# Moving one of the five DMA issues per step pair from GpSimd to SyncE in the second attention of a hybrid block

## The chip, the cores and the metric

One core of a Trainium2 chip runs the whole kernel in one launch. The metric is device time in microseconds (us). A measurement of the kernel is the median of several runs; a profiled execution is one further run, whose trace gives the durations used below.

## The reference, cut to what matters

The input x has 4 batches of 1024 rows of 256 numbers, all in f32. Four layers are added to it in turn, each applied to a layer norm of x: an attention (a), a feed-forward net, a second attention (b) and the same feed-forward net again. "Layer 3" is the second attention.

```
x = x + attn_a(layernorm(x)); x = x + ffn(layernorm(x))
x = x + attn_b(layernorm(x)); x = x + ffn(layernorm(x))

# attn_b(x): 16 heads of 64
h = layernorm(x) * ln_scale + ln_bias
q = (h @ w_down_q.T) @ w_up_q.T ; k, v = from (h @ w_down_kv.T)
q, k = rope(q), rope(k)
out = softmax(q @ k.T / 8) @ v
return out @ w_out.T + x
```

## The kernel before, in words

**Tiling.** An attention is walked in 256 steps: 4 batches, 8 pairs of heads in each, 8 tiles of 128 queries in each pair of heads. A step computes the scores of 128 queries against 1024 keys for two heads, in one PSUM tile `sc` for each head. Two steps, 2h and 2h+1, make a step pair h, and there are 128 step pairs. A period below is the time of one step pair.

**What a step does.** `scores` (L238, TensorE) fills the two `sc` tiles. `exponentials` takes the row maximum (L249, VectorE) and the exponential with its sum (L251, ScalarE) into `p`; `invert` (L259 VectorE, L260 ScalarE) adds the inverse sums to it. `turn` (L271, VectorE) transposes `p` into `T`, but only within blocks of 32x32. To complete the transpose, 16 squares of `T` (a square is 32 partitions x 1088 f32, 136 KB, for a whole step pair) must move to another group of 32 partitions, in a tile `pT`. `send` (L289 to L295) does this with one DMA per square. `weigh` (L304, TensorE) multiplies `pT` with the values, `take` (L314 ScalarE, L316 GpSimd) copies the sums out of PSUM and scales them by the inverse sums, `project` (L167 TensorE, L326 ScalarE, L328 GpSimd) multiplies with the output weights and adds the result to x.

**Squares in layer 3.** `attention` is called with kept=1 there, so the square (0, 0), which stays in its partitions, is copied by ScalarE (`keep`, L287), and 15 squares are left in the list `sent`. SyncE (SP) issues the first ten, GpSimd (POOL) the last five (POOL_DMA = 5). In layer 1, kept is 0 and there are 16: SP issues eleven and GpSimd five.

**Order of the work.** The kernel is scheduled by hand: each engine executes its instructions in the order in which the loop `steps_with` emits them. In a step s that is: `invert(s)`; `scores(s+1)`; if s is even, GpSimd's sends of step pair s/2-1, then `project` of step pair (s-6)/2; `exponentials(s+1, 0)`; if s is odd, `weigh` of step pair (s-5)/2; `exponentials(s+1, 1)`; if s is odd, `take`; `turn(s)`; if s is odd, SP's sends of step pair (s-1)/2. So SP's sends follow straight after the second transpose of a step pair, and GpSimd's come in the next step. `weigh` of a step pair comes four steps after the second transpose.

**Buffers.** `T` and `pT` have two buffers each. `turn(2h+4)`, the first transpose into the buffer of T of step pair h, can start only when all transfers of step pair h have landed. SP's first send of step pair h can start only when `take` of step pair h-2 has read pT (L316). The scores have three PSUM tiles.

**Other work on the two queues.** In layer 3, SP also issues the loads of the next pair of heads' weights: three of `wo` (L212, L214) and three of `w` (L636), once in four step pairs each. GpSimd also does, in nearly every step pair, one block of the rope: two DMAs that swap neighbouring partitions into a tile `turned` (L652), and a step later three elementwise operations (L657, L658, L659), the first of which overwrites what those DMAs read and so waits until they have landed. GpSimd's order in a period is therefore L316, two L652, five L295, L328, L657, L658, L659.

**Completion semaphores.** SP's DMAs take eight completion semaphores in turn, and GpSimd's another eight; an issue waits for the transfer that used its semaphore before.

Of the kernel before, what the change touches and what calls it, by code (L numbers as in the profile page):

```python
# [27 lines left out]
HB = 2  # L28
# [4 lines left out]
POOL_DMA = 5  # L33
# [6 lines left out]
def hybrid_block_kernel(  # L40
# [5 lines left out]
    nc = tc.nc  # L46
# [134 lines left out]
    def attention(prep_batch, prep_pair, wo, loader, lead, kept):  # L181
# [47 lines left out]
        def scores(s):  # L229
            g, qs = steps[s]  # L230
            qT, kT = tiles[g]["qT"], tiles[g]["kT"]
            for j in range(2):
                sc[s, j] = ps_sc.tile([P, S], F32, tag="sc", name="sc")
            for m in range(S // 512):
                for half in range(2):
                    for j in range(2):
                        rows = slice(j * DH, (j + 1) * DH)
                        nc.tensor.matmul(  # L238
                            sc[s, j][ts(half, DH), ts(m, 512)],
                            qT()[rows, ts(2 * qs + half, DH)], kT()[rows, ts(m, 512)],  # L240
                            start=True, stop=True,
                        )

        def exponentials(s, j):
            if j == 0:
                probs[s] = pp.tile([P, NK, NG, SQ], F32, tag="p", name="p")
                total[s] = small.tile([P, 2], F32, tag="total", name="total")
            nmax = small.tile([P, 1], F32, tag="nmax", name="nmax")
            nc.vector.tensor_reduce(nmax, sc[s, j], AX.X, ALU.max, negate=True)  # L249
            place = j ^ (s % HB)  # L250
            nc.scalar.activation(  # L251
                probs[s][:, :NK2, ts(j, 2), :],
                sc.pop((s, j)).rearrange("p (k c i) -> p k c i", c=2, i=SQ), AF.Exp,
                bias=nmax, accum_out=total[s][:, place : place + 1],
            )

        def invert(s):
            t = total.pop(s)
            nc.vector.reciprocal(t, t)  # L259
            nc.scalar.copy(  # L260
                probs[s][:, NK2].rearrange("p (j c) i -> p j (c i)", j=2),
                t.unsqueeze(2).to_broadcast([P, 2, DH]),
            )

        def turn(s):
            h, q = divmod(s, HB)
            if q == 0:
                T[h] = tp.tile([P, SENT], F32, tag="T", name="T").rearrange(
                    "p (c q k i) -> p c q k i", c=NG, q=HB, k=NK
                )  # L270
            nc.vector.transpose(  # L271
                T[h][:, :, q, :, :].rearrange("p c k i -> p k c i"), probs.pop(s)
            )
# [8 lines left out]

        sent = [ac for ac in squares if ac not in [(a, a) for a in range(kept)]]

        def keep(h):
            for a in range(kept):
                nc.scalar.copy(pT[h][ts(a, SQ), a], T[h][ts(a, SQ), a])  # L287

        def send(h, engine, which):  # L289
            if h not in pT:  # L290
                pT[h] = ptp.tile([P, SENT], F32, tag="pT", name="pT").rearrange(
                    "p (a q k i) -> p a q k i", a=NG, q=HB, k=NK
                )
            for a, c in which:
                engine.dma_start(pT[h][ts(c, SQ), a], T[h][ts(a, SQ), c])  # L295

        def weigh(h):

            v = tiles[HB * h // NT]["v"]()
            av[h] = [group(P) for q in range(HB)]  # L300
            for k in range(NK2):
                for q in range(HB):
                    for j in range(2):
                        nc.tensor.matmul(  # L304
                            av[h][q][ts(j ^ q, DH)], v[ts(j, DH), k, :],
                            pT[h][ts(j, DH), :, q, k, :],
                            start=(k == 0), stop=(k == NK2 - 1),
                        )

        def take(h):  # L310

            oT[h] = otp.tile([P, HB, P], F32, tag="oT", name="oT")
            for q, sums in enumerate(av.pop(h)):
                nc.scalar.copy(oT[h][:, q], sums)  # L314
            parts = oT[h].rearrange("p q (a i) -> p a q i", i=SQ)
            nc.gpsimd.tensor_mul(parts, parts, pT.pop(h)[:, :, :, NK2, :])  # L316

        def project(h):
            g, t0 = divmod(HB * h, NT)
            b, pr = pairs[g]  # L320
            po = group(HB, D)
            for t in range(HB):
                paired(po[:, t, :], [(oT[h][:, t], [wos[g][:, t]] * 2)])
            oT.pop(h)
            got = tmp.tile([P, HB, D], F32, tag="tmp", name="got")
            nc.scalar.copy(got, po)  # L326
            xd = xs[b][:, t0 : t0 + HB, :]
            nc.gpsimd.tensor_add(xd, xd, got)  # L328

        def steps_with(others):  # L330
            for k, f in others:
                pieces.setdefault(k, []).append(f)
            for s in range(-1, n + LAG + 1):
                h, part = divmod(s - LAG, HB)
                ahead = 0 <= s + 1 < n
                if 0 <= s < n:
                    invert(s)
                if ahead:
                    scores(s + 1)
                if part == 1 and 0 <= s // HB - 1 < n // HB:  # L340
                    send(s // HB - 1, nc.gpsimd, sent[len(sent) - POOL_DMA :])
                if part == 1 and 0 <= h < n // HB:
                    project(h)
                if ahead:
                    exponentials(s + 1, 0)
                for f in pieces.get(s - EARLY, ()):
                    f()
                if part == 0 and 0 <= h < n // HB:
                    weigh(h)
                if ahead:  # L350
                    exponentials(s + 1, 1)
                if part == 0 and 0 <= h < n // HB:
                    take(h)
                if 0 <= s < n:
                    turn(s)
                if part == 0 and 0 <= s // HB - 1 < n // HB:
                    keep(s // HB - 1)
                    T.pop(s // HB - 1)
                if part == 0 and 0 <= s < n:
                    send(s // HB, nc.sync, sent[: len(sent) - POOL_DMA])  # L360
                for f in pieces.get(s, ()):
                    f()

# [128 lines left out]
    def layer_a():  # L492
# [70 lines left out]
        later = [(4 + i, lambda i=i: rows.measure(2 + i // TQ, i % TQ)) for i in range(6 * TQ)]  # L563
        later += [(4 + 6 * TQ, lambda: rows.finish[2]())]
        first, steps = attention(batch_a, pair_a, wo_a, nc.gpsimd, lead=3, kept=0)
        loads, xn, pair = first[:2], first[2:14], first[14:]

# [16 lines left out]
    def layer_b(rows):  # L584
# [45 lines left out]
        def pair_b(b, pr):  # L630
# [47 lines left out]
            return {name: lambda name=name: made[name] for name in ("qT", "kT", "v")}, load, work  # L678

        return attention(batch_b, pair_b, wo_b, nc.sync, lead=5, kept=1)  # L680


# [73 lines left out]
```

## Time and profile before

| | us |
|---|---|
| median of 3 runs | 3288.75 (3285.65 to 3289.74) |
| profiled execution, its own time | 3283.29 |
| its span, first to last instruction | 3281.4 |
| granted TensorE clock, mean | 0.996 of full speed |

How the page is read: a group's busy time is the union of its instructions, "idle before" is the time in which the engine stood still just before them and what ended that; the chain is followed back from the last instruction to whatever released it. SP has no busy row, since all that it does is waiting and issuing; its rows carry the name SPq. The span has four parts: layer 1 from 0 to about 1480 us, a first feed-forward net to about 1680 us, layer 3 to about 3030 us, and the second feed-forward net to the end. The rows of the page on the transfers are these:

```
pT<-T SPq DMA_DIRECT2D x2688, 136.0 KB, 4.7
pT<-T POOLq DMA_DIRECT2D x1280, 136.0 KB, 4.7
turned<-kT POOLq DMA_DIRECT2D x128, 128.0 KB, 3.5
turned<-qT POOLq DMA_DIRECT2D x128, 128.0 KB, 3.3
```

The first is 128 x 11 of layer 1 and 128 x 10 of layer 3, and the last column is the median time from issue to landing in us.

### The profile page before, as it was taken

To read this page: it belongs to the slowest core of one execution; us is meant where nothing else is said; L and a number is where in the kernel's file an instruction comes from. 1 tells how busy PE (TensorE), PEld (TensorE's weight loads), DVE (VectorE), ACT (ScalarE), POOL (GpSimd) and SP (SyncE) were. 2 spreads that over 40 slices of the span, in tenths; PEclk is the share of its full clock that TensorE was granted. 3 is DMA by queue.
4 is the path that set the end of the run, shared out by engine and by line. 5 is a ranking of instruction groups with operands and counts; after the bars stand their busy time and mean duration, and the time that the engine had idled before them with its cause. 6 is when DMAs were issued, how large, how long until landed. Compare 5 with 4: busy or idle time off the path is not lost.

```text
span 3281.4 us, 126564 instructions
## 1 busy us (share of the span) xinstructions
PE 3201.6 (98%) x52736; PEld 2022.3 (62%) x52736; DVE 2531.3 (77%) x2386; ACT 2109.0 (64%) x4304; POOL 1958.4 (60%) x2738
## 2 busy tenths in 40 slices
PE   8999999999999999999999999999999999998999
PEld 4666666666666666666555556666656666665666
DVE  7988888888888888941049889998989999998100
ACT  5666666666666666642447777777778777777332
POOL 4544454545444445430159888998989999996110
PEclk9999999999999999999999999999999999999999
DMA  8888888888888888840029889998888899998100
GB/s 226 224 220 213 226 223 222 219 227 223 222 214 218 222 229 225 218 116 0 2 81 237 223 217 240 242 240 236 240 229 240 240 243 247 245 246 214 38 20 20
DMA packets 244697, 642.13 MB, mean 196 GB/s; under 512 B 74304, under 2 KB 102976, under 8 KB 244128
## 3 DMA queue, kind: packets, MB, share of 16 engines
q1 hardware_dynamic: 161104, 397.60, 47.6%
q0 software_dynamic: 83024, 236.44, 25.8%
q8 instruction: 419, 6.86, 0.9%
q14 instruction: 150, 1.23, 0.1%
HBM read 43.39 MB, written 4.19 MB: 15 GB/s over the span
## 4 chain that ended last, share of the span: by engine, by line
PE 78%; SPq 8%; DMA 5%; DVE 3%; ACT 3%; issue 3%; POOL 1%; DVEq 0%; POOLq 0%; ACTq 0%
PE sc L238 23%; PE mm L304 21%; PE mm L167 16%; SPq L295 7%; PE mm L421 7%; PE ph L410 7%; PE mm L176 5%; DMA pT<-T 4%; DVE T L271 1%; DVE nmax L249 1%; ACT p L251 1%; PE mm L153 1%; POOL oT L316 0%; ACT gT L414 0%; SPq L214 0%
## 5 line engine op out<-in xcount | busy, mean ns | idle before, releaser
L249 DVE TENSOR_REDUCE nmax<-sc 128x1 f32<-128x1024 f32 x1024 | 1204.5, 1218 | 226.7 <-PE sc L238 223.5
L251 ACT ACTIVATE p<-sc,nmax 128x1024 f32<-128x1024 f32 x1024 | 1145.3, 1119 | 324.0 <-DVE nmax L249 324.0
L271 DVE STREAM_TRANSPOSE T<-p 128x2176 f32<-128x2176 f32 x512 | 1247.1, 2436 | 41.0 <-DMA pT<-T 17.6
L238 PE MATMUL sc<-kT,qT 64*64 64x512 f32 x8192 | 1085.5, 599 | 16.0 <-ACT p L251 10.6
L304 PEld LDWEIGHTS mm<-pT,v 64*64 64x64 f32 x32768 | 950.3, 133 | 145.6 <-issue 103.4
L304 PE MATMUL mm<-pT,v 64*64 64x128 f32 x32768 | 984.5, 269 | 14.5 <-issue 13.5
L295 POOL DMA_DIRECT2D pT<-T x1280 | 629.6, 499 | 121.1 <-PE sc L238 56.2
L316 POOL TENSOR_TENSOR oT<-oT,pT 128x256 f32<-128x256 f32 x256 | 186.1, 727 | 718.7 <-ACT oT L314 636.3
L238 PEld LDWEIGHTS sc<-kT,qT 64*64 64x64 f32 x8192 | 333.1, 133 | 409.9 <-issue 277.1
L328 POOL TENSOR_TENSOR x<-x,got 128x512 f32<-128x512 f32 x256 | 330.9, 1293 | 27.8 <-ACT got L326 23.9
L326 ACT COPY got<-mm 128x512 f32<-128x512 f32 x256 | 150.0, 586 | 283.0 <-PE mm L167 282.9
L428 DVE TENSOR_TENSOR x<-x,mm 128x512 f32<-128x512 f32 x32 | 22.0, 687 | 367.2 <-PE mm L421 367.1
L167 PE MATMUL mm<-wo,oT 128*64 128x256 f32 x2048 | 278.4, 393 | 19.6 <-POOL oT L316 18.6
L167 PEld LDWEIGHTS mm<-wo,oT 128*64 128x64 f32 x2048 | 124.6, 136 | 266.4 <-POOL oT L316 217.4
L414 ACT ACTIVATE gT<-ph,b_sb 128x512 f32<-128x512 f32 x128 | 87.5, 686 | 301.9 <-PE ph L410 301.8
L260 ACT COPY p<-total 128x128 f32<-128x128 f32 x512 | 151.8, 296 | 195.4 <-DVE total L259 188.5
L167 PE MATMUL mm<-hT,w 128*64 128x512 f32 x1024 | 242.9, 596 | 1.0 <-ACT hT L156 1.0
L421 PE MATMUL mm<-w_sb,gT 128*128 128x256 f32 x1024 | 226.0, 381 | 6.6 <-ACT hT L156 6.6
L410 PE MATMUL ph<-hT,w_sb 128*128 128x512 f32 x512 | 230.2, 603 | 0.5 <-ACT hT L156 0.5
L421 PEld LDWEIGHTS mm<-w_sb,gT 128*128 128x128 f32 x1024 | 193.1, 190 | 39.4 <-ACT hT L156 9.4
L396 POOL TENSOR_TENSOR x<-x,b_sb 128x256 f32<-128x256 f32 x64 | 44.5, 728 | 275.6 <-ACT xn L147 275.6
L251 ACT ACTIVATION_READ_ACCUMULATOR p<-sc,nmax 128x1 f32 x1024 | 205.3, 200 | 0.0
(90 smaller groups left out, 2473.1 us busy)
## 6 DMA issues: line engine op xcount, KB each, us to landing
pT<-T SPq DMA_DIRECT2D x2688, 136.0 KB, 4.7
pT<-T POOLq DMA_DIRECT2D x1280, 136.0 KB, 4.7
turned<-kT POOLq DMA_DIRECT2D x128, 128.0 KB, 3.5
turned<-qT POOLq DMA_DIRECT2D x128, 128.0 KB, 3.3
w<-in_wqkv_a POOLq DMA_DIRECT2D x96, 128.0 KB, 6.1
wo<-in_wo_a POOLq DMA_DIRECT2D x32, 128.0 KB, 5.4
wo<-in_wo_a POOLq DMA_DIRECT2D x64, 64.0 KB, 5.5
wo<-in_wo_b SPq DMA_DIRECT2D x32, 128.0 KB, 3.6
```

The lines of the kernel that those rows point to most:

```text
L167: nc.tensor.matmul(out[ts(j, DH)], lhsT[:, ts(j, DH)], rhs[j], start=(first and i == 0), stop=(last and i == len(parts) - 1),)
L176: nc.tensor.matmul(out[ts(j, DH)], lhsT, rhs[:, ts(j, DH)], start=(i == 0), stop=(i == len(parts) - 1),)
L238: nc.tensor.matmul(sc[s, j][ts(half, DH), ts(m, 512)], qT()[rows, ts(2 * qs + half, DH)], kT()[rows, ts(m, 512)], start=True, stop=True,)
L249: nc.vector.tensor_reduce(nmax, sc[s, j], AX.X, ALU.max, negate=True)
L251: nc.scalar.activation(probs[s][:, :NK2, ts(j, 2), :], sc.pop((s, j)).rearrange("p (k c i) -> p k c i", c=2, i=SQ), AF.Exp, bias=nmax, acc ...
L271: nc.vector.transpose(T[h][:, :, q, :, :].rearrange("p c k i -> p k c i"), probs.pop(s))
L295: engine.dma_start(pT[h][ts(c, SQ), a], T[h][ts(a, SQ), c])
L304: nc.tensor.matmul(av[h][q][ts(j ^ q, DH)], v[ts(j, DH), k, :], pT[h][ts(j, DH), :, q, k, :], start=(k == 0), stop=(k == NK2 - 1),)
L316: nc.gpsimd.tensor_mul(parts, parts, pT.pop(h)[:, :, :, NK2, :])
L328: nc.gpsimd.tensor_add(xd, xd, got)
L410: nc.tensor.matmul(ph, w1_sb[:, c, ts(f, P)], hT[n][:, c, :], start=(c == 0), stop=(c == NC - 1),)
L421: nc.tensor.matmul(po[n][:, t % 2, :], gT[n][:, f, ts(t, P)], w2_sb[:, f, :], start=(f == 0), stop=(f == NF - 1),)
```

## The change

The number of squares that GpSimd sends is POOL_DMA less the number of squares that ScalarE keeps. In layer 1 this is still five. In layer 3 it is four, and SP sends eleven. The square that changes its queue is the eleventh of the list `sent`, from partitions 64 to 95 to partitions 32 to 63; SP issues it straight after its ten others, where GpSimd issued it first of its five in the next step. Nothing else moves on any engine; SP's first send of a step pair waits for four of GpSimd's completion semaphores in place of five.

```diff
         sent = [ac for ac in squares if ac not in [(a, a) for a in range(kept)]]
 
+        by_pool = POOL_DMA - kept
+
...
                 if part == 1 and 0 <= s // HB - 1 < n // HB:
-                    send(s // HB - 1, nc.gpsimd, sent[len(sent) - POOL_DMA :])
+                    send(s // HB - 1, nc.gpsimd, sent[len(sent) - by_pool :])
...
                 if part == 0 and 0 <= s < n:
-                    send(s // HB, nc.sync, sent[: len(sent) - POOL_DMA])
+                    send(s // HB, nc.sync, sent[: len(sent) - by_pool])
```

## The prediction

> **What bounds the kernel now.** The change touches layer 3 alone, so I read the page first for what TensorE does over the span, then the window of layer 3 by itself (1700 to 2980 us, 122 periods of 10.5 us), then the waits of that window engine by engine, and last the records of the two queues. The page and the window, whose columns are PE, PEld, DVE, ACT and POOL busy, then clock, DMA share and GB/s:
>
> ```profile
> PE 3201.6 (98%) x52736; PEld 2022.3 (62%) x52736; DVE 2531.3 (77%) x2386; ACT 2109.0 (64%) x4304; POOL 1958.4 (60%) x2738
> ...
> PE 78%; SPq 8%; DMA 5%; DVE 3%; ACT 3%; issue 3%; POOL 1%; DVEq 0%; POOLq 0%; ACTq 0%
> ```
>
> ```profile
> 1700.00:2980.00 1280.00, 1245.70 (x23037) 784.18 (x23035) 1167.95 (x1014) 979.32 (x1961) 1136.93 (x1476) 0.99 0.89 237
> ```
>
> TensorE is busy for 1245.7 of 1280 us here: 34.3 us are all that any relief of another engine could give in this window. GpSimd (89%), VectorE (91%) and the DMA engines (0.89) are close behind, so the stage is nearly balanced. SP has no busy figure; summed from its records in the window it is 1189 us: 979.9 for 1215 sends of squares (mean 0.806), 117 for weight loads, some 90 for the gaps of 0.045 between instructions and for passed waits. That is 9.75 us a period, 93%, and leaves 0.74 us idle. Its issues and GpSimd's, by duration (min/median/max, ns):
>
> ```profile
> L295 SPq DMA_DIRECT2D pT<-T x1215: 507/598/2159, 1700.0 to 2976.9; - x174
> ```
>
> ```profile
> L295 POOL DMA_DIRECT2D pT<-T x605: 489/492/522, 1710.2 to 2975.3; - x152
> ```
>
> SP's shortest issues are near 0.59, and the mean is higher because the third to sixth of each ten take 0.83 to 1.08: these fall in the time of GpSimd's five. GpSimd's never lengthen. Now who waits, first TensorE, then GpSimd, then SP, then VectorE:
>
> ```profile
> PE mm L167 <- POOL oT L316: 15.4, 23, 3.3
> ```
>
> ```profile
> POOL kT L657 <- DMA turned<-kT: 8.9, 13, 1.1
> POOL qT L657 <- DMA turned<-qT: 8.3, 10, 1.4
> ```
>
> ```profile
> SPq L295 <- DVE total L259: 60.7, 51, 3.3
> SPq L295 <- POOL oT L316: 14.5, 14, 3.5
> ```
>
> ```profile
> DVE nmax L249 <- PE sc L238: 61.5, 109, 2.7
> ...
> DVE T L271 <- DMA pT<-T: 8.5, 11, 2.0
> ```
>
> About half of TensorE's idle time is for L316, the scaling on GpSimd; SP mostly waits for the transpose (named "total", the last instruction of the same semaphore); VectorE waits little for landings. The chain puts SP and the landings at 28% of this window. I discount that: many of its hops go from a landing to L316, but L316 reads a pT that `weigh` has already read in whole, and GpSimd's records show it busy without a gap up to such an L316. These hops are the last use of a shared semaphore, not a wait.
>
> **What GpSimd gains.** One issue of 0.492 us less in each of 128 step pairs, 63 us off its queue. Most has no one waiting. In the window, 13 of TensorE's gaps before L167 come with an L316 that started over 0.15 us after ScalarE's copy was done, because GpSimd was still at work; they sum to 12.4 us. (The other ten or so, 0.3 us each, have GpSimd waiting, and gain nothing.) One issue less starts L316 up to 0.49 us earlier, unless L657 must wait for the swapped tile:
>
> ```profile
> 2077.95 1.14 POOL L652 DMA_DIRECT2D turned<-kT  x2
> 2079.08 2.43 POOL L295 DMA_DIRECT2D pT<-T  x5
> 2081.53 1.28 POOL L328 TENSOR_TENSOR x<-x,got 128x512 f32<-128x512 f32 x1
> 2083.94 1.27 POOL L657 TENSOR_TENSOR kT<-kT,cos_sb 128x512 f32<-128x512 f32 x1 [1.13 <-DMA turned<-kT]
> ```
>
> The five sends and L328 are what covers the flight of the two swaps, 3.3 to 3.5 us. Here the cover was 1.13 us too short, and a shorter send row only lengthens that wait. Over 121 rotations of layer 3, 26 wait so now, and with 0.49 us less cover 61 would: in half the periods part of the gain or all of it is lost. Taking for each of the 13 gaps the least of 0.49 us, the gap itself and the cover to spare leaves 4.3 us: seven gaps with the whole 0.49, two with 0.36 and 0.46, four with nothing. I take -3 us, since the freed time is partly limited by what is next late (SP, or the transpose); the ends are 0 and -7 (all 13 gaps and the one at 2982 us, 0.49 us each at most).
>
> **What SP pays.** One more issue at the tail of its row. The nearest row is its tenth in layer 3, mean 0.788 us, with 0.045 of gap 0.83; the eleventh of layer 1's rows is near it, 0.727. Against this GpSimd's burst is one shorter. The ten issues of a row take 8.10 us, 2.2 more than ten of 0.59; put down to GpSimd's five, that is 0.44 each, and by issues three to six alone (1.5 us over 0.59 in all) 0.30. So the row lengthens by 0.83 less 0.30 to 0.44, about +0.45 us. The bounds are +0.1 (the transfer engines, not the issue, pace the row, and the 15 transfers are the same) and +0.83 (nothing comes back).
>
> Two statements of the Trainium skill, page "DMA: Bandwidth & Descriptors", speak for making the move freely. "Issuing engine by pattern" calls the hardware queue of SP generally faster than GpSimd's; the row differs here, 0.806 us against 0.492 an issue. "Issuing engines are not separate DMA queues" says that all queues end on the same 16 engines, and that the issue time saved by spreading is usually small beside the transfer. The first half would make the landing of the last square unchanged: cost 0. The second half doesn't hold here: in the window the DMA engines move 237 GB/s, so 136 KB takes 0.59 us at that rate, no more than its issue on SP. By the page the sum is -3 us; by the rows SP's queue is itself a resource with 0.74 us left, and the price below is added. I follow the rows.
>
> **Where the longer row goes.** Two things are queued behind it on SP: the weight loads, needed long after, and the next row. A row starts late when SP is still at work: now in the median 0.65 us after the transpose, where 0.13 is the least, and 1.1 to 1.2 us in the periods after loads. With 0.45 us more of work the idle 0.74 shrinks to about 0.3, and such lateness grows by some 0.3. So the last landing of a step pair, now in the median 12.3 us after the transpose, moves by 0.75 to 0.8. Who needs it? `weigh` starts 3.0 us after it (5% of the pairs: 0.6), so it hardly notices. The first transpose into the same T buffer, L271, starts 1.0 us after it, in 5% of the pairs 0.1 to 0.2. Shifting each of 115 step pairs' landings by 0.8 us gives VectorE 21 us of new waits. VectorE has 112 us idle in the window, 61.5 of them waiting for scores, and 6 of the 21 disappear there. Of the 15 left, most are covered too, because the PSUM tile that VectorE and ScalarE then free is needed only after a `weigh` of 3.5 us: subtracting the margin between each exponential's end and the scores that reuse its tile leaves 4.9 us on TensorE. The same working gives 1 us at a shift of 0.4, 14 at 1.2 and 25 at 1.5: cheap at first, steep past one microsecond.
>
> **Sum.** -3 from GpSimd, +5 from SP: +2 us. Against the profiled execution, 3283.3 becomes 3285.3. That execution lies 5.5 us under the median of the three runs, so the forecast is 3288.75 + 2, about 3291.
>
> **The rivals.** A measurement of this kernel can tell about 0.2%, 6.6 us, from no change.
>
> *Absorbed both ways* (likeliest, 0.50): the sum above, from -4 (shift 0.3, the whole of GpSimd's gain) to +6. About 3291.
>
> *SP becomes the bound* (0.38): the row lengthens by the full 0.83 us, so that SP needs 9.75 + 0.83 = 10.6 us a period where the others need 10.5; the place is the first transpose of a step pair on VectorE, waiting for the eleventh square. The point from which it decides is a growth of 0.74 us a row, SP's idle time. It then costs 0.1 us in each of 128 periods, 13 us, and with the shift of 1.2 us (14 us) to 1.5 us (25 us) less GpSimd's 3, between 8 and 22: about 3302. For it speaks that SP's work is uneven (loads of 1.6 to 1.9 us in every second period), so that it runs out of slack there first; against it, that the burst which slows SP shrinks.
>
> *GpSimd's relief wins* (0.12): SP's row grows by only 0.1, the transposes wait for nothing new, and the lateness that GpSimd carries over from one period to the next shrinks by more than one issue each time, -7 to -10: about 3281. For it speaks the row "PE mm L167 <- POOL oT L316", the largest of TensorE's waits; against it, the lost cover of the swaps.
>
> That the change doesn't do what it says is excluded by the order of instructions: GpSimd loses 128 issues and SP gains 128.
>
> **How the numbers follow.** The forecast is 3291, of the absorbed case, whose own range is 3284 to 3296. The range that should hold 8 in 10 must reach into the SP case and need not hold the fast one: 3283 to 3308. Faster by over 0.2% means under 3282.2, slower over 3295.3. So faster 0.12, same 0.50, slower 0.38.
>
> **What would show it.** In layer 3 after: SP's sends 11 a period with a mean near 0.77 us and SP's waits for the transpose down from 61 us to 20 to 40; the waits of L657 for the swaps up from 17 us to about 35; TensorE's waits for L316 down from 15 to about 11; the waits of L271 for landings up from 8.5 to some 25; TensorE's idle time in the window within 10 us of 34. It is wrong if SP no longer waits for the transpose at all (then the SP case holds), if the mean of SP's issues stays at 0.806 (the burst was not what slowed them), or if L316 is no longer late while L271's waits stay (then the fast case).

## The result and the profile after

The change makes the kernel slightly slower: the median is 3295.93 us (3294.42 to 3302.12, 6 runs) against 3287.2 us for the kernel before, measured beside it (3283.74 to 3293.35, 6 runs). The ratio is 1.0032, with a 95% interval of 1.0020 to 1.0044: some 7 to 14 us. This is above the 0.2% from which the forecast speaks of slower, and inside the range of 3283 to 3308, but it is not the case that was called likeliest.

In the profiled execution (3295.33 us, span 3293.4 us) layer 3 runs from its first to its last transpose in 1359.2 us, before in 1346.3 us. Layer 1 is unchanged (1394.4 us, before 1394.6). All of the difference lies where the change was made. L295 is now L297, L304 L306, L316 L318, and L657 L659. From the page, busy time by engine and the chain:

```profile
PE 3212.3 (98%) x52736; PEld 2019.1 (61%) x52736; DVE 2530.4 (77%) x2386; ACT 2105.6 (64%) x4304; POOL 1898.1 (58%) x2610
...
PE 64%; SPq 20%; DMA 5%; issue 4%; ACT 3%; DVE 3%; POOL 1%; ACTq 0%; DVEq 0%; POOLq 0%
```

GpSimd is busy for 60 us less, and SP's share of the chain has gone from 8% to 20%: the longest path now runs through SP's row of sends for longer stretches. The window of layer 3, with the columns of before:

```profile
1700.00:2980.00 1280.00, 1244.90 (x22816) 772.70 (x22814) 1154.87 (x1001) 964.79 (x1937) 1071.78 (x1344) 1.00 0.87 235
```

TensorE's busy time is that of before, 1245 us, but it got through 22816 matmuls in place of 23037, 1% less. So the loss does not show as idle time at all; more on that below. The two queues, with min/median/max in ns:

```profile
L297 SPq DMA_DIRECT2D pT<-T x1325: 507/594/2202, 1699.4 to 2979.8; - x190
L297 POOL DMA_DIRECT2D pT<-T x480: 489/493/520, 1709.6 to 2973.0; - x160
```

And the waits of the same window, for SP, VectorE, GpSimd and TensorE:

```profile
SPq L297 <- DVE total L259: 24.5, 26, 3.0
SPq L297 <- DMA pT<-T: 4.9, 11, 0.8
SPq L297 <- POOL oT L318: 4.2, 9, 0.9
```

```profile
DVE nmax L249 <- PE sc L238: 49.7, 99, 1.7
DVE T L271 <- DMA pT<-T: 32.4, 22, 3.6
```

```profile
POOL kT L659 <- DMA turned<-kT: 23.2, 26, 1.9
POOL qT L659 <- DMA turned<-qT: 14.6, 17, 1.7
```

```profile
PE mm L167 <- POOL oT L318: 14.6, 36, 1.8
PE sc L238 <- ACT p L251: 9.2, 11, 2.9
```

SP waits less for the transpose, so it has less room. VectorE's transpose waits almost four times as long for landings (8.5 us before). GpSimd waits twice as long for its swaps (17.2 us before). TensorE's waits for L318 fell by 0.8 us only.

**Where TensorE's time went.** A matmul of the scores is in flight for 0.6 us in the mean, and the next ones start before it ends, so a wait shorter than that need not leave a gap in TensorE's busy time. What does show it is the time from the start of one matmul to the start of the next. Summed over layer 3 by what the two matmuls belong to (worked out from the records; "scores to project" is the step from the last matmul of the scores to the first of `project`, and so holds the waits for GpSimd's scaling; smaller steps are left out), in us:

| | before | change |
|---|---|---|
| within `weigh` | 456.0 | 453.2 |
| within the scores | 389.3 | 401.4 |
| scores to `project` | 86.1 | 87.0 |
| `weigh` to scores | 21.4 | 24.9 |
| scores to `weigh` | 50.6 | 52.0 |
| layer 3 in all | 1346.3 | 1359.2 |

The scores take 12.1 us longer. Inside a step's 16 score matmuls, TensorE waits for the PSUM tile that ScalarE's exponential must free. The row of TensorE's weight loads shows the same wait, first before, then after:

```profile
PEld sc L238 <- ACT p L251: 45.8, 56, 3.8
```

```profile
PEld sc L238 <- ACT p L251: 59.3, 71, 3.8
```

### The profile page after: what moved, and what is told of

It is laid out like the page before. It is cut to its first block, busy times and chain, and to the rows that moved or that the text cites. A ratio compares the mean times of both kernels' runs of the same rounds, so it can differ in the third digit from the quotient of the medians.

```text
span 3293.4 us, 126436 instructions
## 1 busy us (share of the span) xinstructions
PE 3212.3 (98%) x52736; PEld 2019.1 (61%) x52736; DVE 2530.4 (77%) x2386; ACT 2105.6 (64%) x4304; POOL 1898.1 (58%) x2610
## 4 chain that ended last, share of the span: by engine, by line
PE 64%; SPq 20%; DMA 5%; issue 4%; ACT 3%; DVE 3%; POOL 1%; ACTq 0%; DVEq 0%; POOLq 0%
SPq L297 19%; PE sc L238 17%; PE mm L306 16%; PE mm L167 13%; PE mm L423 7%; PE ph L412 7%; DMA pT<-T 4%; PE mm L176 4%; ACT p L251 1%; DVE nmax L249 1%; DVE T L271 1%; POOL oT L318 1%; SPq L214 1%; SPq L638 1%; PE mm L153 0%
## 5 line engine op out<-in xcount | busy, mean ns | idle before, releaser
L271 DVE STREAM_TRANSPOSE T<-p 128x2176 f32<-128x2176 f32 x512 | 1247.5, 2436 | 73.4 <-DMA pT<-T 39.4
L238 PE MATMUL sc<-kT,qT 64*64 64x512 f32 x8192 | 1091.8, 598 | 20.1 <-ACT p L251 14.8
L306 PEld LDWEIGHTS mm<-pT,v 64*64 64x64 f32 x32768 | 947.4, 133 | 149.1 <-issue 99.7
L306 PE MATMUL mm<-pT,v 64*64 64x128 f32 x32768 | 986.1, 269 | 12.4 <-issue 8.9
L297 POOL DMA_DIRECT2D pT<-T x1152 | 568.1, 500 | 118.7 <-PE sc L238 54.9
L318 POOL TENSOR_TENSOR oT<-oT,pT 128x256 f32<-128x256 f32 x256 | 186.0, 727 | 770.7 <-ACT oT L316 692.4
L330 POOL TENSOR_TENSOR x<-x,got 128x512 f32<-128x512 f32 x256 | 330.8, 1292 | 27.5 <-ACT got L328 23.7
L167 PE MATMUL mm<-wo,oT 128*64 128x256 f32 x2048 | 278.4, 393 | 19.0 <-POOL oT L318 17.3
L167 PEld LDWEIGHTS mm<-wo,oT 128*64 128x64 f32 x2048 | 124.6, 136 | 267.2 <-POOL oT L318 223.0
L167 PE MATMUL mm<-hT,w 128*64 128x512 f32 x1024 | 244.2, 598 | 1.2 <-ACT hT L156 1.2
```

The lines of the kernel that those rows point to most:

```text
L167: nc.tensor.matmul(out[ts(j, DH)], lhsT[:, ts(j, DH)], rhs[j], start=(first and i == 0), stop=(last and i == len(parts) - 1),)
L238: nc.tensor.matmul(sc[s, j][ts(half, DH), ts(m, 512)], qT()[rows, ts(2 * qs + half, DH)], kT()[rows, ts(m, 512)], start=True, stop=True,)
L271: nc.vector.transpose(T[h][:, :, q, :, :].rearrange("p c k i -> p k c i"), probs.pop(s))
L306: nc.tensor.matmul(av[h][q][ts(j ^ q, DH)], v[ts(j, DH), k, :], pT[h][ts(j, DH), :, q, k, :], start=(k == 0), stop=(k == NK2 - 1),)
```

## The experiments

The theory: the cost comes through SP's queue. SP's longer row of sends delays the last landing of a step pair, so the next transpose into that T buffer waits, the row maxima and exponentials behind it are late, and the scores wait for a PSUM tile. GpSimd's relief pays part of it back. Three rivals: the transfer engines are what is paid (136 KB in another place), GpSimd's lost cover for the swaps is what is paid, or only the sum of SP's work counts and not its distribution. Ratios are to the kernel before, run on the same chip, with 95% intervals; 0.1% is 3.3 us. A trace is of one execution of each kernel. Layer 1, which no edit touches, takes 1391.8 to 1400.7 us in these traces, so differences of a few us between two kernels are read from layer 3 alone where that can be done.

**extra_sp: one more issue on SP, without data.** In the kernel before, behind SP's sends (`spare` is a new tile that nothing reads):

```diff
                     send(s // HB, nc.sync, sent[: len(sent) - POOL_DMA])
+                    if kept:
+                        nc.sync.dma_start(spare[:SQ, s // HB % 16 : s // HB % 16 + 1], eps[:SQ])
```

> The kernel before, with one more issue on SP after its ten sends in each step pair of layer 3: a transfer of 128 bytes to a tile that nothing reads. GpSimd keeps its five. If SP's queue time is the cost (the longer row delays the last landing and so the next transpose), this costs about what the change costs or somewhat more, since GpSimd's burst is as long as before: +8 to +16 us, SP's waits for the transpose down to 20 to 30 us from 61 in the window of layer 3. If the cost of the change is in the 136 KB that go another way, this costs nothing: within 3 us of the kernel before.

Measured: 1.0087 (1.0074 to 1.0100), some 29 us. So an issue alone costs, without the 136 KB:

```profile
L364 SPq DMA_DIRECT2D spare<-eps x119: 507/591/1644, 1707.5 to 2977.1; - x119
```

This issue of 128 bytes takes 0.59 us in the median, as long as one of 136 KB. SP's waits for the transpose fell to 10.8 us. The scores took 404.3 us (+15.0) and the steps from scores to `project` 94.7 (+8.6). The turn of the completion semaphores can be little of it: all of SP's waits for landings are 9.5 us in the window, against 5.0 before. The theory held in kind, but the price was twice what it said: 29 us, where the change itself costs about 10.

**act_from_pool and after_loads_act: relieving SP by ScalarE's queue.** Both start from the changed kernel. In the first ScalarE issues the moved square, and in the second all weight loads of layer 3:

```diff
-                    send(s // HB, nc.sync, sent[: len(sent) - by_pool])
+                    send(s // HB, nc.sync, sent[: len(sent) - POOL_DMA])
+                    if kept:
+                        send(s // HB, nc.scalar, sent[len(sent) - POOL_DMA : len(sent) - by_pool])
```

```diff
-                    nc.sync.dma_start(w[:, i], up[:, ts(pr, P)])
+                    nc.scalar.dma_start(w[:, i], up[:, ts(pr, P)])
...
-        return attention(batch_b, pair_b, wo_b, nc.sync, lead=5, kept=1)
+        return attention(batch_b, pair_b, wo_b, nc.scalar, lead=5, kept=1)
```

> The changed kernel, but ScalarE issues the moved square and SP keeps ten: GpSimd's relief alone, with the shorter cover for the swaps. If SP's queue is the cost, this is -1 to -5 us against the kernel before (the 3 us of GpSimd, less some for one more issue on ScalarE). If the lost cover of the swaps on GpSimd is the cost, +8 us stays.

> The changed kernel with the loads of layer 3's weights (six issues in four step pairs) on ScalarE's queue in place of SP's. SP is relieved by some 0.85 us a period, more than the change adds. If SP's queue time is the cost, the time falls back to the kernel before or below it: 0 to -6 us against before, and SP waits for the transpose again for over 60 us. If the transfer engines or GpSimd's cover are the cost, +8 us stays.

Measured: 1.0024 (1.0013 to 1.0035) and 1.0234 (1.0221 to 1.0248), 8 and 77 us. Both missed what the theory said. The 8 us of the first are what the rival of the lost cover said, but neither run tells the theories apart, for they brought a wait of their own. SP's waits in after_loads_act:

```profile
SPq L297 <- DMA pT<-T: 66.9, 101, 1.8
SPq L297 <- DVE total L259: 57.1, 48, 3.0
SPq L297 <- DMA wo<-in_wo_b: 53.0, 28, 4.3
SPq L297 <- DMA w<-in_wuq: 43.2, 28, 4.9
```

In the program's order of instructions, SP's and ScalarE's transfers take the same eight completion semaphores in turn. A load that stands behind exponentials in ScalarE's queue is issued late, and SP's send that comes next to the same semaphore waits until it has landed: 96 us in the last two rows, which are absent from the waits of the change, where SP issues the loads itself. In act_from_pool the same showed as 45.5 us of SP's waits for "DMA pT<-T", and the swaps waited 62 us.

**pool6: the opposite move,** six squares on GpSimd and nine on SP.

```diff
-        by_pool = POOL_DMA - kept
+        by_pool = POOL_DMA + kept
```

> The opposite move: GpSimd six squares, SP nine in layer 3. If SP's queue and GpSimd's lateness both have a price, the kernel before stands near the best split: the landings come 0.5 us earlier (-2 us) and L316 is late more often (+6): 0 to +7 us. If the change costs only through SP and GpSimd has room, this is faster by 3 to 8 us. If the lost cover of the swaps was the cost, the longer cover here makes it faster by 3 us or more, with the waits for the swaps near 5 us in place of 17.

Measured: 1.0005 (0.9998 to 1.0013), 2 us, as the first case has it. The swaps waited 6 us and the transposes for landings 5.6 us, both less than before, so the lost cover alone is not what counts; but in the window L318 was late 27 times by 30.5 us in all, against 20 times and 17.5 us before, and scores to `project` took 93.5 us (+7.4).

**extra_pool and after_extra_pool: the price of GpSimd's queue.** One more issue of 128 bytes ahead of GpSimd's sends, in the kernel before and in the changed one; in the second GpSimd then has five issues again, and only SP's side of the change is left.

```diff
+                    if kept:
+                        nc.gpsimd.dma_start(spare[:SQ, s // HB % 16 : s // HB % 16 + 1], eps[:SQ])
                     send(s // HB - 1, nc.gpsimd, sent[len(sent) - POOL_DMA :])
```

> The kernel before, with one more issue on GpSimd ahead of its five sends in each step pair of layer 3: a transfer of 128 bytes to a tile that nothing reads, about 0.5 us of its queue. This prices GpSimd's time. If it is worth as little as the prediction has it (3 us for 0.49 us a period, part of it paid back by a longer cover for the swaps): +2 to +5 us. If GpSimd's time is worth as much as SP's, as the gap between the change (+9) and one more issue on SP alone (+28) suggests: +8 to +15 us.

> The changed kernel with the same small issue on GpSimd, so that GpSimd has five issues again and only SP's side of the change is left. By the prediction's 3 us: +10 to +13 us against before. If GpSimd's relief is worth the gap between the change and one more issue on SP alone: +18 to +28 us.

Measured: 1.0065 (1.0052 to 1.0078) and 1.0074 (1.0060 to 1.0089), 21 and 24 us. The issue takes 0.505 us. The rows of TensorE's waits for the scaling (L318, or L320), in extra_pool and in after_extra_pool:

```profile
PE mm L169 <- POOL oT L318: 28.1, 41, 2.2
```

```profile
PE mm L169 <- POOL oT L320: 19.5, 42, 2.0
```

With 15.4 us before and 14.6 in the change, half a microsecond of GpSimd is seen to cost TensorE in this place in both kernels. In extra_pool the steps from scores to `project` take 100.9 us, 14.8 more than before, of the 17.6 that layer 3 grew. The longer burst also delays the squares that SP sends: their last landing comes 12.9 us after the transpose, against 12.5 before (means, worked out from the records), and VectorE waits longer for landings than the 8.5 us before, first in extra_pool, then in after_extra_pool (32.4 in the change):

```profile
DVE T L273 <- DMA pT<-T: 19.8, 21, 2.3
```

```profile
DVE T L273 <- DMA pT<-T: 36.8, 25, 3.3
```

So GpSimd's 0.5 us a period is worth more than 3 us. Given back to GpSimd in the changed kernel, it costs 14 us by the ratios (0.42%, from 1.0032 to 1.0074, two intervals that don't touch) and 11 by layer 3 of the traces; added to the kernel before, it costs 21 us by the ratio, and in the traces 18 in layer 3 and 6 in layer 1, where nothing was changed.

**pool3: one step further,** twelve on SP and three on GpSimd (`by_pool = POOL_DMA - 2 * kept`).

> One step further: GpSimd three squares, SP twelve in layer 3. SP had 0.33 us a period idle with eleven; a twelfth adds about 0.5 to 0.6. If SP's queue is the cost it is now the bound: its waits for the transpose near zero, the period 10.75 to 10.9 us, +20 to +40 us. If the cost of a square on SP is linear: +17 us.

Measured: 1.0113 (1.0096 to 1.0130), 37 us, steeper than linear. The period is 10.88 us in the profiled execution, which took 11 us longer than the other three. SP's waits for the transpose are down to 17.7 us, and VectorE's for landings are the longest of its waits:

```profile
DVE T L271 <- DMA pT<-T: 53.8, 25, 5.2
DVE nmax L249 <- PE sc L238: 39.2, 83, 2.0
```

**before_noload and after_noload: SP without the weight loads.** Both load functions return early, with the first pair's tile:

```diff
+            if kept and g:
+                wos[g] = wos[0]
+                return
...
+                if ws:
+                    made["w"] = ws[0]
+                    return
```

> The kernel before, where layer 3 loads the weights of the first pair of heads only and uses them for all pairs (both loads, w and wo, are left out for the others). SP has 0.83 us a period less to issue. Theory: SP's queue is the cost. Then this shows what SP's queue cost already before: -2 to -8 us. Rival, the shorter cover of the swaps on GpSimd is the cost: within 3 us of before.

> The changed kernel with the same loads left out. Theory: SP then has more room than before the change, and the difference between change and no change disappears or turns: between -4 and +2 us against the same kernel with ten and five. Rival: the lost cover on GpSimd is untouched, so +7 to +10 us stays between the two.

Measured: 1.0040 (1.0027 to 1.0052) and 0.9969 (0.9959 to 0.9980). The rival is out: between the two the change is a gain of 0.7%, where it should have cost 7 to 10 us. But the theory's number for before_noload was wrong in sign. SP waits 190 us for the transpose there and the transposes wait 2.7 us for landings, yet the kernel is 13 us slower. TensorE's longest waits, in before_noload and in after_noload:

```profile
PE mm L307 <- issue: 20.4, 16, 2.4
PE mm L167 <- POOL oT L319: 10.6, 15, 3.3
```

```profile
PE mm L309 <- issue: 13.2, 13, 2.0
PE mm L167 <- POOL oT L321: 8.7, 16, 1.5
```

"issue" is a pause, here inside `weigh`, for which the profile has no wait. All pauses of this kind over 0.3 us in layer 3, in `weigh` or in the scores (10 before, 9 in the change, 28 and 16 here; 11.3, 5.4, 30.1 and 15.1 us), end 1.2 to 1.7 us after a packet of the larger queue of kind "instruction" ended, though such packets are 7 us apart in the mean. That points to TensorE waiting for its own instructions, which is argued from this regularity and not tested. The pauses account for 18.8 of the 19.9 us that layer 3 grew in before_noload, and for 15 of the 23 us between the two kernels; without them the change is still a gain of some 9 us there. They also hide part of the change itself: without them layer 3 grew by 18.9 us, not 12.9. Whether the kernel or the single execution makes them more or less frequent stays open.

**before_spread and after_spread: the same loads, one or two ahead of each row** in place of three ahead of every second, with `load` and `load_out` taking the part to load:

```diff
-                pieces.setdefault(NT * g - NT - lead - EARLY, []).append(load)
-            pieces.setdefault(NT * g - 1 - EARLY, []).append(lambda g=g: load_out(g))
+                for i in range(3) if kept else (None,):
+                    pieces.setdefault(NT * g - NT - lead - EARLY + 2 * (i or 0), []).append(
...
+            for i in range(3) if kept else (None,):
+                pieces.setdefault(NT * g - 1 - EARLY + 2 * (i or 0), []).append(
...
```

> The kernel before, with the six loads of four step pairs spread over them (one or two ahead of each row of sends, where it was three ahead of every second). The work on SP is the same, only more even. Theory: the rows after loads no longer start 1.1 us late, and the transposes wait less: -1 to -4 us. If only the sum of SP's work counts, nothing: within 1 us.

> The changed kernel with the loads spread in the same way. Theory: more of its cost disappears than before_spread gains, since it has less slack: 3 to 7 us less than the change, so +2 to +6 us against the kernel before. If only the sum of SP's work counts, +8 to +10 us stays.

Measured: 1.0001 (0.9991 to 1.0011) and 1.0000 (0.9991 to 1.0009). The change costs nothing once the loads are spread, more than expected, and before gains nothing. In the traces layer 3 takes 1347.3 us in after_spread, against 1359.2 in the change. That the sum of SP's work alone counts is out. So are the other two rivals as the main cost: the square goes the same way as in the change, and the swaps wait 34 us, against 38 there, yet nothing is lost. The reason given is half confirmed: the rows start as late as in the change (1.06 us after the transpose, mean; 1.05), but VectorE's idle time before the first transpose of a step pair fell from 57.8 us in layer 3 to 43.3. What fell on TensorE is spread over several rows: scores to `project` 83.4 us (87.0 in the change), the scores 399.1 (401.4), `weigh` 451.4 (453.2).

**after_spread_wo_pool: the attempt at a better version,** after_spread with the wo loads on GpSimd behind its swaps (the loader is nc.gpsimd and the three parts of load_out are placed at NT * g - 1 + 2 * i).

> The changed kernel with the w loads spread as before (one in each of three step pairs) and the wo loads, spread too, on GpSimd just behind its swaps, where they restore the cover that the moved square took away. SP has 0.4 us a period less than in the changed kernel, GpSimd 0.1 less than before. If both queues have a price, this is the best of them: -8 to 0 us against before.

Measured: 1.0015 (1.0007 to 1.0023), a miss. GpSimd's price is paid again: 20.0 us of TensorE's gaps stand before L167, against 15.6 in after_spread (its traced execution is the slowest of 22). No version that does the whole computation beat the kernel before.

## Why the prediction was half right

**SP's row: right.** It grew from 8.53 to 9.12 us, by 0.59 where 0.45 was taken (bounds 0.1 and 0.83). The mean issue fell to 0.781 us (near 0.77 was said), with one square fewer on GpSimd; SP's idle time fell from 0.73 to 0.33 us a period (about 0.3); its waits for the transpose to 24.5 us (20 to 40); the swaps wait 38 us (about 35); L271 waits 32.4 us for landings (some 25). One step was off: the last landing of a step pair moved by 0.35 us (12.46 to 12.81, means), not by 0.75 to 0.8, because the last transfer lands 2.65 us after the end of its issue, where it took 3.16; without GpSimd's relief (after_extra_pool) it moved by 0.63.

**What this does to TensorE: the place right, the size wrong.** The step that failed is "leaves 4.9 us on TensorE". With GpSimd's relief taken away SP's side costs 24 us (after_extra_pool), and one more bare issue on SP 29. Both parts of that term were mis-sized. First, VectorE's new waits were put at 21 us. Its idle time just before the first transposes of the step pairs, whatever ended it, summed over layer 3 from the records, is 25.9 us before, 57.8 in the change, 66.5 in after_extra_pool and 79.9 in extra_sp. One reason is that the 21 us let a transpose start almost at once after the last landing (redone from the records: 20 us at once, 28 us at the least delay on record, 0.12 us). A transpose into a used T buffer has some thirteen semaphores to check, and its records show them taken two at a time, 0.1 us apart; in the 38 first transposes of the change with a wait over 0.3 us, the start came 0.51 us after the last landing in the median. The margin to the landing, read as 1.0 us, is 0.8 in the records. With 0.5 us for the checks and the shift of 0.63, the margins of the kernel before give an estimate of 40 us of new waits, and after_extra_pool shows 41; for the change itself the same sum gives 18, and 32 were measured, so it is not the whole account.

Second, of the 21 us a quarter was let through to TensorE ("most are covered too"). In after_extra_pool layer 3 grew by 24.1 us on 41 of new waits, and in extra_sp by 28.4 on 54: over half. Which of the margins between an exponential and the next scores failed to cover them is not resolved.

**GpSimd's relief: too small by a factor of about four or more.** The step "I take -3 us" counted TensorE's gaps before L167, and allowed 7 us at most. Taking the relief away costs 11 to 14 us, and adding half a microsecond to the kernel before 18 to 21. The sign it named did not come: TensorE's waits for L316 stayed at 14.6 us, where 11 was said. Left out were what GpSimd's burst does to SP's landings (12.5 to 12.9 us in extra_pool), and that a late L316 also holds up SP's sends of the step pair after next (SP's waits for it: 14.5 us before, 23.7 in extra_pool, 4.2 in the change). Waits for L316 too short to leave a gap may add to it; their share is not shown.

**The sum** was therefore +24 less 14 by the ratios, and not +5 less 3: two errors of one kind, which cancelled in part. That the time fell inside the range is to that extent luck. The statement behind both, "34.3 us are all that any relief of another engine could give", does not hold as a bound, nor as the sign it was used for: TensorE's idle time in the window stayed at 35 us while layer 3 grew by 12.9 us, so time is lost, and can be won, without idle time. Of the rivals, the one in which SP becomes the bound came nearest: SP did not run out (0.33 us left), but the cost was paid at the place named there, the first transpose of a step pair. The decision by the rows, against the Trainium skill's sentence that issue time is usually small beside the transfer ("DMA: Bandwidth & Descriptors", "Issuing engines are not separate DMA queues"), held: one more SP issue of 128 bytes in each step pair of layer 3 costs 29 us.

## What to carry to other kernels

In this kernel several queues and engines are busy for some 90% of a period, and half a microsecond of queue time per period had a price on both queues (a sixth to a third of itself). Moving an issue gives only the difference of two such prices, so measure both by adding a transfer of a few bytes to one queue and to the other before moving a real one. And price a wait of TensorE by the spacing of matmul starts, by stretch, not by its idle time; waits shorter than a matmul's flight (0.6 us for the scores here) need not appear there.

## What the runs showed of the hardware

An issue on SP takes as long for 128 bytes (median 0.591 us) as for 136 KB (0.596), and one on GpSimd too (0.505 and 0.492). SP's mean issue falls with the number of squares that GpSimd sends meanwhile: 0.861 us at six, 0.806 at five, 0.781 at four and 0.744 at three; a small fifth issue in place of a square leaves it at 0.777. A transpose that waits for some thirteen semaphores starts 0.51 us (median) after the last landing. And TensorE's pauses without a wait, 5 to 30 us of layer 3, end 1.2 to 1.7 us after a packet of an instruction queue and differ from trace to trace, which is enough to hide or feign an effect of a few microseconds.
